# A two-layer attention and mixture-of-experts kernel: transposes in place of identity products, one-hot products on VectorE, expert numbers found earlier, loads of t ahead of a branch, more filler matmuls

## The chip, the core and the metric

The kernel runs on one core of one Trainium2 chip. The metric is the device time of one execution in microseconds (us); the time given is the median of several executions. A profile of one execution is read beside it. The engines are called as the profile calls them: PE is TensorE's matmul, PEld its weight load, DVE is VectorE, ACT is ScalarE, POOL is GpSimd, SP is SyncE, which here issues most DMAs.

## The reference

The input x is one image of 256 channels and 48 by 48 pixels, so 2304 tokens of 256 channels, all in float32. The reference computes:

```python
# layer 0: group norm, then softmax attention over tokens x heads (9216 rows of 64)
xt = gn(x).transpose(0, 2, 3, 1)
q, k, v = xt @ Wq.T + bq, xt @ Wk.T + bk, xt @ Wv.T + bv      # each as [9216, 64]
O = softmax(q @ k.T / 8, axis=1) @ v
x = x + (O.reshape(B, H, W, 256) @ Wo.T + bo)
# layer 1, attention through 64 slices
t = tokens(x); h = ln(t) @ W0 + b0
sw = softmax(h @ Ws + bs)                                      # [tokens, 64]
# q, k, v of h averaged over tokens with weights sw, attention among the 64 slices (8 heads of 32),
# result spread back to the tokens with sw, then @ Wout + bout
t = t + that
# layer 1, mixture of experts
xf = ln(t); top 2 of 8 experts by xf @ Wg, softmax over the two
for e in range(8): out += w_dense[:, e:e+1] * (gelu(xf @ W1[e] + b1[e]) @ W2[e] + b2[e])
t = t + out
```

The result is t as an image again, 256 by 48 by 48.

## The kernel before

The function `layers` computes everything and leaves t, one row a token, in a DRAM tensor `t_d`. The entry function calls it once, reads a flag `bad`, calls it again (with row maxima in the softmax) only if the flag is set, and then turns t into the image. Tile inserts the waits; operations issued through the small wrapper `InOrder` (`pe`, `dve`, `act`, `pool`; all of these show as L57) keep the order in which they are written on their engine, and those issued as `nc.tensor...` or `nc.vector...` may be moved by the scheduler.

**Projections.** x is loaded as [128, 2, 2304] (`x_sb`, channels on partitions). `transposed` turns a 256 by 256 weight with four PE transposes and copies the result with ACT. `Wq` and `Wk` are turned first; then DVE takes the statistics of x, PE sums them over groups with two small matmuls (`pg`, `pg2`) with DVE and POOL work between, one transpose `pb` turns the biases, and the normalized x (`xn`, which lies in the memory of `t_sb`) feeds the matmuls for q and k (L287, L291) in five blocks of tokens. The scheduler placed the transposes of `Wv` between `pb` and the first q matmul and those of `Wo` after the first block. The v matmuls (L316) follow.

**Attention.** 18 blocks of 512 rows of q run over 36 pairs of key tiles: `scores` (L57, `s<-q,kk`), an exponential on ACT, row sums on DVE, and `times_values` (`av<-p,v_sb`). `follow` puts the later steps of a finished token tile between two blocks: `out_proj` computes, in the PSUM tile `pa`, the output projection of the tile and adds x by multiplying `x_sb` with an identity; `turn`, `slices` and `gather` follow one block later each. The last two tiles are done after the loop, in tiles named `pm`. `busy(n, bank)` issues n matmuls [128x128] by [128x256] whose result nobody reads.

**Slices.** A chain of small matmuls and DVE/ACT steps between 64 slices ends in `tw`; two `busy(1, spin)` stand in it. Then each token tile gets its share added (`py`), with statistics, logits of the experts and the normalized t written to DRAM (`tn_d`).

**Routing.** DVE picks two experts for each token, counts them and gives each (token, expert) pair a slot in one of 43 tiles of 128 rows (`NSL`); each tile has one expert. The table from slot to token comes from one-hot products. For every column k of 36, `in_tile` (DVE, L57, 18 columns at a time) marks the tile, `what` (POOL, 9 columns at a time, 774 values) is `in_tile` times token and weight, `in_row` (DVE, 9 columns, 1152 values, printed as `t_sb<-row,back` since it lies in that memory) marks the row; PE adds up the products in `pwide` (`pw<-what,t_sb`). After that DVE counts, for each tile, how many experts end before it (`past`, `ex`), writes `expert_i` and `used_i` (integers), and turns the table into `slot_t` and `slot_w`.

**Experts.** For each tile s, POOL gathers its 128 rows of `tn_d` (`rows`, L1060, `xs`), SP loads the expert's W1 (`load_w1`, L1070, 1 MB, two buffers), PE turns xs (`turn`), `first` makes 1024 hidden values with ACT's gelu, `second` the output, and POOL adds it into `t_d` with an indirect DMA (L1120). 36 tiles are always run; the other seven stand in nested branches on `used_i`. In the profiled execution 39 ran. `expert_of` reads `expert_i` into a register.

**End.** All engines read `bad` and branch. The branch not taken has a short path on each engine that waits for the engine's and its DMA queues' counts and then raises them to what the skipped part would have left. Then SP loads t in five blocks of up to 512 tokens (`tt<-t_d`), PE turns them (L1209), DVE and ACT copy (`ob`), SP stores. The pool `fin` has five buffers of `tt` and five of `ob`.

Of the kernel before, what the change touches and what calls it, by code (L numbers as in the profile page):

```python
# [9 lines left out]
FP = mybir.dt.float32  # L10
# [5 lines left out]
P = 128  # L16
C = 256
# [26 lines left out]
def bc(ap, shape):  # L44

    return ap.unsqueeze(2).to_broadcast(shape)
# [16 lines left out]
def layers(  # L63
# [168 lines left out]
    with proj, tc.tile_pool(name="ps_pj", bufs=5, space=PSUM) as ps_pj, tc.tile_pool(  # L232
        name="ps_w", bufs=2, space=PSUM
    ) as ps_w:
        def transposed(dst, raw):
            pw = ps_w.tile([P, 2, C], FP, name="pw", tag="pw")
            for ci in range(2):
                for co in range(2):
                    nc.tensor.transpose(
                        pw[:, ci, co * P : (co + 1) * P], raw[:, co, ci * P : (ci + 1) * P], ident  # L240
                    )
            nc.scalar.copy(dst, pw)
            return dst

        WqT = transposed(pj.tile([P, 2, C], FP, name="WqT"), raws["Wq"])
        WkT = transposed(pj.tile([P, 2, C], FP, name="WkT"), raws["Wk"])

# [8 lines left out]
        nc.tensor.matmul(pg[:, 0:2], gm, mv[:, :, 0], start=True, stop=True)  # L256
# [7 lines left out]
        nc.tensor.matmul(pg2[:, 0:2], gm, dm, start=True, stop=True)  # L264
# [4 lines left out]
        nc.tensor.transpose(pb[:, 0:76], brow, ident[0:76, 0:76])  # L269
        nc.vector.tensor_copy(bcol, pb[:, 0:76])  # L270
        bq8 = pj.tile([P, 2], FP, name="bq8")
# [108 lines left out]
    def out_proj(i, ps):  # L380

        tok = slice(i * P, (i + 1) * P)
        g, u = divmod(i, TG // P)
        for c in range(2):
            pe.matmul(
                ps[:, 0:C], OT[:, g % 2, c, u * P : (u + 1) * P], WoT[:, c, :],
                start=(c == 0), stop=False,
            )
        for c in range(2):
            pe.matmul(  # L390
                ps[:, c * P : (c + 1) * P], x_sb[:, c, tok], ident, start=False, stop=(c == 1)
            )

        def add():
            dve.tensor_tensor(t_sb[:, i, 0:C], ps[:, 0:C], bo_bc, ALU.add)

        def spread():
            s6 = small.tile([P, 6], FP, name="s6", tag="s6")
            dve.bn_stats(s6, t_sb[:, i, 0:C])
            dve.bn_aggr(stats[:, i, :], s6)  # L400
            ve = small.tile([P, 1], FP, name="ve", tag="ve")
            dve.tensor_scalar(ve, stats[:, i, 1:2], 1e-5, None, ALU.add)
            pool.tensor_tensor(rstd_t[:, i : i + 1], ve, mhalf[:, 0:1], ALU.pow)
            return ve

        def norm():
            dve.tensor_scalar(
                tn[:, i % 6, :], t_sb[:, i, 0:C], stats[:, i, 0:1], rstd_t[:, i : i + 1],
                ALU.subtract, ALU.mult,
            )  # L410

        return [(2, add), (3, spread), (7, norm)]
# [69 lines left out]
    def attention():  # L482


        with tc.tile_pool(name="pexp", bufs=5) as pexp, tc.tile_pool(
            name="att", bufs=2
# [231 lines left out]
    with tc.tile_pool(name="sa", bufs=1) as sa:  # L718
        tw = sa.tile([P, C + E], FP, name="tw")
        with sums_done, tc.tile_pool(name="ps_b", bufs=3, space=PSUM) as ps_b, tc.tile_pool(  # L720
# [81 lines left out]
            for v in range(2):  # L802
                pa = ps_b.tile([S, 2, P], FP, name="pa", tag="mm")
                for u in range(2):
                    pe.transpose(pa[:, u, :], a[:, v, u, :], ident)
                if v == 0:
                    dve.tensor_copy(aT[:, v], pa)
                else:
                    act.copy(aT[:, v], pa)
            dve.tensor_reduce(am, a, AX.X, ALU.add)  # L810
            dve.reciprocal(am, am)
            pk = ps_b.tile([P, 4, D1], FP, name="pk", tag="mm")
            for v in range(2):
                for u in range(2):
                    for w in range(2):
# [4 lines left out]
                        )  # L820
            tok_sb = sa.tile([P, 4, D1], FP, name="tok_sb")
# [34 lines left out]
        with tc.tile_pool(name="ps_y0", bufs=7, space=PSUM) as ps_y0, tc.tile_pool(  # L856
            name="norm", bufs=2
# [40 lines left out]
    with gating, tc.tile_pool(name="onehot", bufs=1) as oh, tc.tile_pool(  # L898
# [100 lines left out]

        for k in range(0, K, G):  # L1000
# [3 lines left out]
            pool.tensor_tensor(  # L1004
# [6 lines left out]
            )  # L1011
        for j in range(K):
# [7 lines left out]

        past = gp.tile([P, NSL, E], FP, name="past")
        dve.tensor_tensor(
            past, bc(steps[:, 0:NSL], [P, NSL, E]), ends.unsqueeze(1).to_broadcast([P, NSL, E]), ALU.is_ge
        )
        ex = gp.tile([P, NSL], FP, name="ex")
        dve.tensor_reduce(ex, past, AX.X, ALU.add)
        dve.tensor_scalar(expert_i, ex[0:1, :], float(E - 1), None, ALU.min)
        dve.tensor_scalar(used_i, ends[0:1, E - 1 : E], float(NSL), None, ALU.min)
# [147 lines left out]
def kernel(ctx: ExitStack, tc: tile.TileContext, *args):  # L1176
    nc = tc.nc
    out_v = args[-1][0].rearrange("(c p) h w -> p c (h w)", p=P)
    both = ctx.enter_context(tc.tile_pool(name="both", bufs=1))
    bad = both.tile([1, 1], mybir.dt.int32, name="bad")  # L1180
    ident = both.tile([P, P], FP, name="ident")
# [3 lines left out]
    layers(tc, bad, ident, t_d, *args[:-1])  # L1185
    again = nc.values_load(
# [4 lines left out]


    sp = InOrder(tc, nc.sync)
    with tc.tile_pool(name="fin", bufs=len(TBLOCKS)) as fin, tc.tile_pool(
        name="ps_f", bufs=4, space=PSUM
    ) as ps_f:
        tts = []
        for t0, n in TBLOCKS:
            tt = fin.tile([P, 4, C], FP, name="tt", tag="tt")
            tts.append(tt)  # L1200
            sp.dma_start(
                out=tt[:, 0 : n // P, :], in_=t_d[t0 : t0 + n, :].rearrange("(i p) c -> p i c", p=P)
            )
# [48 lines left out]
```

## Time and profile before

| | us |
|---|---|
| median of 3 executions | 1629.55 |
| lowest, highest | 1628.57, 1630.72 |
| profiled execution | 1630.58 |
| its span, first to last instruction | 1628.8 |

| engine | busy us | share of the span |
|---|---|---|
| PE | 1573.0 | 97% |
| DVE | 1047.5 | 64% |
| ACT | 810.4 | 50% |
| POOL | 149.7 | 9% |

Approximate stages in the profiled execution: projections until 66 us, attention until 1243, slices until 1282, routing until 1317, experts until 1605, end until 1628.8. Busy time counts an instruction from start to end; PE's instructions overlap, so the spacing of starts tells the cost better than the duration. PEclk (and "granted clock") is the share of full TensorE clock that the chip granted. An arrow in a line names what ended the idle time before it.

### The profile page before, as it was taken

How to read it: one execution, taken by the hardware profiler on the slowest of the kernel's cores; microseconds unless marked ns; L12 is line 12 of the kernel's file. 1: busy time of each engine (PE TensorE's matmuls, PEld its weight loads, DVE VectorE, ACT ScalarE, POOL GpSimd, SP SyncE). 2: the span in 40 equal slices, each digit the busy share in tenths (PEclk: the TensorE clock that was granted, in tenths of full speed). 3: DMA queues.
4: the chain of work that ended last, by engine and by line, in shares of the span. 5: the costliest groups of instructions: out<-in, count | busy, mean ns of one | idle time of the engine just before them, and what ended most of it. 6: DMA issues, size and time to landing. Idle time of an engine off the chain costs nothing.

```text
span 1628.8 us, 31884 instructions
## 1 busy us (share of the span) xinstructions
PE 1573.0 (97%) x13244; PEld 792.2 (49%) x13244; DVE 1047.5 (64%) x1364; ACT 810.4 (50%) x1100; POOL 149.7 (9%) x129
## 2 busy tenths in 40 slices
PE   7999999999999999999999999999999689999995
PEld 3633343333333333333333333333345479999994
DVE  6577778777787887877878878778786721111111
ACT  2355565555555655655556556555553322333321
POOL 0000000000000000000000000000000253333321
PEclk9999999999999999999999999999999799999998
DMA  4000000000000000000000000000003656666655
GB/s 136 1 1 1 1 1 1 1 1 1 1 1 1 2 1 2 1 1 2 1 1 1 1 1 1 1 1 1 1 2 117 232 180 190 173 183 188 172 161 174
DMA packets 39877, 79.26 MB, mean 49 GB/s; under 512 B 3581, under 2 KB 26186, under 8 KB 39594
## 3 DMA queue, kind: packets, MB, share of 16 engines
q1 hardware_dynamic: 32042, 66.35, 12.1%
q0 software_dynamic: 7680, 10.75, 3.7%
q8 instruction: 108, 1.77, 0.4%
q14 instruction: 47, 0.39, 0.1%
HBM read 64.64 MB, written 12.45 MB: 47 GB/s over the span
## 4 chain that ended last, share of the span: by engine, by line
PE 92%; DVE 3%; DMA 2%; issue 1%; POOL 1%; ACT 0%; SPq 0%; ACTq 0%; POOLq 0%; DVEq 0%
PE s L57 34%; PE av L57 34%; PE ph L57 8%; PE py L57 8%; PE pa L57 2%; DMA t_d<-y,slot_t 2%; PE pb L57 1%; PE pp L287 1%; PE pp L316 1%; PE pp L291 1%; PE pt L57 1%; POOL what L57 0%; DVE s L57 0%; DMA Wq_raw<-in_L_conv_Wq_dram 0%; ACT p L57 0%
## 5 line engine op out<-in xcount | busy, mean ns | idle before, releaser
L57 DVE TENSOR_TENSOR acc<-acc,p 128x1024 f32<-128x1024 f32 x612 | 748.0, 1222 | 256.4 <-ACT p L57 248.3
L57 ACT ACTIVATE p<-s 128x1024 f32<-128x1024 f32 x648 | 662.9, 1023 | 493.3 <-PE s L57 483.2
L57 PE MATMUL av<-p,v_sb 64*64 64x512 f32 x5184 | 675.8, 590 | 1.4 <-ACT p L57 0.7
L57 PE MATMUL s<-q,kk 64*64 64x512 f32 x5184 | 674.9, 589 | 0.0
L57 PEld LDWEIGHTS s<-q,kk 64*64 64x64 f32 x5184 | 201.9, 133 | 351.3 <-issue 181.0
L57 PEld LDWEIGHTS av<-p,v_sb 64*64 64x64 f32 x5184 | 195.8, 131 | 358.1 <-ACT p L57 202.5
L57 ACT ACTIVATE hid<-ph,bcol 128x128 f32<-128x128 f32 x312 | 89.2, 368 | 220.0 <-PE ph L57 209.7
L57 PEld LDWEIGHTS ph<-xT,w 128*128 128x128 f32 x1248 | 147.7, 195 | 2.8 <-DVE xT L57 0.9
L57 PE MATMUL ph<-xT,w 128*128 128x128 f32 x1248 | 148.1, 278 | 0.5 <-DVE xT L57 0.5
L57 PE MATMUL py<-w_sb,hid 128*128 x624 | 147.1, 379 | 0.0
L57 POOL TENSOR_TENSOR rstd_t<-ve,mhalf 128x1 f32<-128x1 f32 (+1 forms) x21 | 27.6, 1312 | 1241.9 <-DVE ve L57 1241.9
L57 DVE COPY xT<-pt 128x256 f32<-128x256 f32 x40 | 17.0, 425 | 175.9 <-PE pt L57 168.6
L57 PEld LDWEIGHTS py<-w_sb,hid 128*128 128x128 f32 x624 | 112.8, 190 | 12.2
L1120 POOL DMA_INDIRECT t_d<-y,slot_t x39 | 61.7, 1583 | 98.7 <-DVE y L57 88.3
L57 DVE TENSOR_TENSOR y<-py,b_bc 128x256 f32<-128x256 f32 x39 | 16.6, 425 | 68.6 <-PE py L57 68.6
L1060 POOL DMA_INDIRECT xs<-tn_d,slot_t x36 | 38.3, 1064 | 91.5 <-PE pt L57 83.5
L57 DVE RECIPROCAL rinv<-pb 128x256 f32<-128x256 f32 x18 | 31.5, 1751 | 0.0
L57 DVE TENSOR_TENSOR acc<-p 128x1024 f32<-128x1024 f32 x18 | 22.1, 1225 | 8.4 <-ACT p L57 8.4
L304 DVE TENSOR_SCALAR q<-pp,bcol 64x512 f32<-64x512 f32 (+1 forms) x30 | 20.8, 694 | 8.6 <-PE pp L287 8.3
L57 DVE TENSOR_REDUCE up<-av 128x512 f32<-128x1024 f32 x18 | 21.9, 1217 | 0.0
L287 PE MATMUL pp<-t_sb,WqT 128*128 128x512 f32 (+1 forms) x40 | 19.0, 600 | 0.3 <-DVE t_sb L278 0.3
L1209 PE MATMUL pt<-ident,tt 128*128 128x128 f32 x36 | 5.8, 340 | 12.8 <-DMA tt<-t_d 12.8
(258 smaller groups left out, 616.6 us busy)
## 6 DMA issues: line engine op xcount, KB each, us to landing
w<-in_L_ffn_W_dram SPq DMA_DIRECT2D x40, 1024.0 KB
w_sb<-in_L_ffn_W_dram SPq DMA_DIRECT2D x8, 1024.0 KB
x_sb<-in_x_dram SPq DMA_DIRECT2D x4, 576.0 KB
t_d<-t_sb SPq DMA_DIRECT2D x3, 768.0 KB
tn_d<-tn SPq DMA_DIRECT2D x3, 768.0 KB
tt<-t_d SPq DMA_DIRECT2D x4, 512.0 KB
out_dram<-ob SPq DMA_DIRECT2D x4, 512.0 KB
b_bc<-in_L_ffn_b_dram SPq DMA_DIRECT2D x1, 1024.0 KB
```

The costliest lines, as they stand in the source:

```text
L57: return self.tc.keep_in_program_order(getattr(self.engine, name)(*args, **kwargs))
L287: nc.tensor.matmul(pq[:, 0:tn], WqT[:, c, cols], xn[:, c, toks], start=(c == 0), stop=(c == 1))
L291: nc.tensor.matmul(pk[:, 0:tn], WkT[:, c, cols], xn[:, c, toks], start=(c == 0), stop=(c == 1))
L304: nc.vector.tensor_scalar(dst, pq[rows, 0:tn], bcol[rows, B_Q + m : B_Q + m + 1], 0.125, ALU.add, ALU.mult,)
L316: nc.tensor.matmul(pv[:, 0:C], xn[:, c, i * P : (i + 1) * P], WvT[:, c, :], start=(c == 0), stop=(c == 1),)
L1060: nc.gpsimd.indirect_dma_start(out=xs, out_offset=None, in_=tn_d[:, :], in_offset=bass.IndirectOffsetOnAxis(ap=slot_t[:, s : s + 1], axis= ...
L1120: nc.gpsimd.indirect_dma_start(out=t_d[:, :], out_offset=bass.IndirectOffsetOnAxis(ap=slot_t[:, s : s + 1], axis=0), in_=y, in_offset=None ...
L1209: nc.tensor.transpose(pt[:, k * P : (k + 1) * P], tt[:, k, c * P : (c + 1) * P], ident)
```

## The change

- `transposed` and the small matmuls of the projections go through `pe`, so PE runs them in the written order: the transposes of Wv and Wo both stand after the first block. `busy_first` adds one filler matmul after `pg` and two after `pb`, into a PSUM bank of its own.
- `out_proj` turns x with two PE transposes that open the accumulation, and the projection is added after.
- Two more `busy(1, spin)` in the slices' chain: after the transposes of `a`, and after `pk`.
- `what` is computed on DVE. The experts' numbers are found inside that loop, on one partition: one DVE compare after the first nine columns, then three adds and two copies on POOL.
- The loads of t are issued before `bad` is read, and again inside the branch. `ob` has three buffers.
- Pools are smaller in the second call of `layers`, which isn't run with these inputs.

```diff
@@ projections
-                    nc.tensor.transpose(
+                    pe.transpose(
                         pw[:, ci, co * P : (co + 1) * P], raw[:, co, ci * P : (ci + 1) * P], ident
...
+        spun = ps_spun.tile([P, 256], FP, name="spun")
+        def busy_first(n):
+            for _ in range(n):
+                pe.matmul(spun, ident, raws["Wq"][:, 0, :], start=True, stop=True)
...
-        nc.tensor.matmul(pg[:, 0:2], gm, mv[:, :, 0], start=True, stop=True)
+        pe.matmul(pg[:, 0:2], gm, mv[:, :, 0], start=True, stop=True)
+        busy_first(1)
...
-        nc.tensor.transpose(pb[:, 0:76], brow, ident[0:76, 0:76])
+        pe.transpose(pb[:, 0:76], brow, ident[0:76, 0:76])
         nc.vector.tensor_copy(bcol, pb[:, 0:76])
+        busy_first(2)
@@ out_proj
+        for c in range(2):
+            pe.matmul(
+                ps[:, c * P : (c + 1) * P], x_sb[:, c, tok], ident, start=(c == 0), stop=False,
+                is_transpose=True,
+            )
         for c in range(2):
             pe.matmul(
                 ps[:, 0:C], OT[:, g % 2, c, u * P : (u + 1) * P], WoT[:, c, :],
-                start=(c == 0), stop=False,
-            )
-        for c in range(2):
-            pe.matmul(
-                ps[:, c * P : (c + 1) * P], x_sb[:, c, tok], ident, start=False, stop=(c == 1)
+                start=False, stop=(c == 1),
             )
@@ slices
+            busy(1, spin)
             dve.tensor_reduce(am, a, AX.X, ALU.add)
...
+            busy(1, spin)
             tok_sb = sa.tile([P, 4, D1], FP, name="tok_sb")
@@ routing
+        past = gp.tile([1, NSL, E], FP, name="past")
+        pool.memset(past, 0.0)
+        def find_experts():
+            dve.tensor_tensor(
+                past[:, :, 0 : E - 1], bc(steps[0:1, 0:NSL], [1, NSL, E - 1]),
+                ends[0:1, 0 : E - 1].unsqueeze(1).to_broadcast([1, NSL, E - 1]), ALU.is_ge,
+            )
+            for n in (4, 2, 1):
+                pool.tensor_tensor(past[:, :, 0:n], past[:, :, 0:n], past[:, :, n : 2 * n], ALU.add)
+            pool.tensor_copy(expert_i, past[:, :, 0])
+            pool.tensor_copy(used_i, ends[0:1, E - 1 : E])
         for k in range(0, K, G):
...
-            pool.tensor_tensor(
+            dve.tensor_tensor(
                 what[:, ks], in_tile[:, ks, :].unsqueeze(2).to_broadcast([P, G, 2, NSL]),
...
+            if k == 0:
+                find_experts()
...
-        past = gp.tile([P, NSL, E], FP, name="past")
-        dve.tensor_tensor(
-            past, bc(steps[:, 0:NSL], [P, NSL, E]), ends.unsqueeze(1).to_broadcast([P, NSL, E]), ALU.is_ge
-        )
-        ex = gp.tile([P, NSL], FP, name="ex")
-        dve.tensor_reduce(ex, past, AX.X, ALU.add)
-        dve.tensor_scalar(expert_i, ex[0:1, :], float(E - 1), None, ALU.min)
-        dve.tensor_scalar(used_i, ends[0:1, E - 1 : E], float(NSL), None, ALU.min)
@@ end
+    tts = [both.tile([P, n // P, C], FP, name=f"t{t0}") for t0, n in TBLOCKS]
+    def load_t():
+        for (t0, n), tt in zip(TBLOCKS, tts):
+            sp.dma_start(out=tt, in_=t_d[t0 : t0 + n, :].rearrange("(i p) c -> p i c", p=P))
+    load_t()
     again = nc.values_load(
         bad, min_val=0, max_val=1, skip_runtime_bounds_check_because="it is the result of a comparison"
     )
     with tc.If(again > 0):
         layers(tc, None, ident, t_d, *args[:-1])
-    with tc.tile_pool(name="fin", bufs=len(TBLOCKS)) as fin, tc.tile_pool(
+        load_t()
+    with tc.tile_pool(name="fin", bufs=3) as fin, tc.tile_pool(
         name="ps_f", bufs=4, space=PSUM
     ) as ps_f:
-        tts = []
-        for t0, n in TBLOCKS:
-            tt = fin.tile([P, 4, C], FP, name="tt", tag="tt")
-            tts.append(tt)
-            sp.dma_start(
-                out=tt[:, 0 : n // P, :], in_=t_d[t0 : t0 + n, :].rearrange("(i p) c -> p i c", p=P)
-            )
```

## The prediction, on record before the changed kernel ran

> **What bounds the kernel now.** I read the page's chain first, then the timeline of the stages that the change touches, then their granted clock, then the end. By engine the chain is:
>
> ```profile
> PE 92%; DVE 3%; DMA 2%; issue 1%; POOL 1%; ACT 0%; SPq 0%; ACTq 0%; POOLq 0%; DVEq 0%
> ```
>
> PE carries the time. Over 66 to 1236 us the waits of PE add up to 1.1 us, so a PE instruction taken out of attention is its spacing saved. Outside attention other things end last. PE between two blocks:
>
> ```profile
> 713.09 0.61 PE L57 MATMUL pa<-ident,x_sb 128*128 128x128 f32 x4
> 713.53 0.38 PE L57 MATMUL pa<-ident,tn 128*128 128x128 f32 x2
> 713.75 0.61 PE L57 MATMUL pb<-Wl,tnT 128*128 128x128 f32 x4
> ```
>
> Two products with an identity are four records, started over 0.44 us; two transposes are two records, over 0.22 us. The clock, in windows of 3.41 us set on the edges at which it changed (columns: window; PE, PEld, DVE, ACT, POOL busy; granted clock; DMA share; GB/s):
>
> ```profile
> 12.35:15.77 3.42, 2.33 (x8) 1.72 (x9) 2.02 (x10) 0.73 (x2) 0.73 (x1) 1.00 0.55 135
> 15.77:19.18 3.41, 3.41 (x5) 1.34 (x5) 1.90 (x5) 0.00 (x0) 0.00 (x0) 1.00 0.75 234
> 1261.63:1265.04 3.41, 2.56 (x26) 1.42 (x26) 1.64 (x5) 1.15 (x3) 0.00 (x0) 1.00 1.09 348
> 1265.04:1268.45 3.41, 3.41 (x8) 2.35 (x10) 0.43 (x1) 0.00 (x0) 0.00 (x0) 0.50 1.09 350
> 1312.83:1316.24 3.41, 0.00 (x0) 0.00 (x0) 0.00 (x0) 0.00 (x0) 2.50 (x4) 1.00 1.02 413
> 1316.24:1319.66 3.42, 2.37 (x10) 1.97 (x11) 0.42 (x1) 0.00 (x0) 2.74 (x3) 0.50 0.57 183
> ```
>
> After a window with gaps the next is granted half the clock (1265, 1316). The 1.00 before 19.18 only means that no record stands there: the q matmuls start 0.853 us apart until 18.95 and 0.43 after. Routing and the first expert tile (SPq w: loads of W1):
>
> ```profile
> 1294.85 0.96 DVE L57 TENSOR_TENSOR in_tile<-first_slot,at_big 128x774 f32<-128x774 f32 x1
> 1295.73 3.91 DVE L57 TENSOR_TENSOR t_sb<-row,back 128x1152 f32<-128x1152 f32 x2
> 1296.04 4.95 POOL L57 TENSOR_TENSOR what<-in_tile,wk 128x774 f32<-128x774 f32 x2 [9.77 <-DVE in_tile L57]
> 1299.57 2.25 DVE L57 TENSOR_TENSOR in_tile<-first_slot,at_big 128x774 f32<-128x774 f32 x1
> 1308.97 15.91 SPq L1070 DMA_DIRECT2D w<-in_L_ffn_W_dram  x3
> 1310.35 1.34 POOL L1060 DMA_INDIRECT xs<-tn_d,slot_t  x1 [3.37 <-DVE slot_w L57]
> 1317.98 6.25 PE L57 MATMUL ph<-xT,w 128*128 128x128 f32 x32 [0.52 <-DVE xT L57]
> ```
>
> DVE and POOL exclude each other: the first in_row runs 1.35, the second 2.64, ending 1.21 after POOL's first what (1298.43); in_tile takes 0.96 alone and 2.25 behind POOL. So the loop is serial: 12.1 us from 1294.85 to 1306.98, of which 1.34 for each what. And the first gather, issued at 1310.35, lands at 1316.7, when two loads of W1 issued since 1308.97 have drained (1316.5). PE stands idle 4.0 us, goes to half clock, and the first tile takes 6.25 where later ones take 3.73. The end:
>
> ```profile
> 1612.16 2.78 SPq L57 DMA_DIRECT2D tt<-t_d  x5
> 1616.54 5.82 PE L1209 MATMUL pt<-ident,tt 128*128 128x128 f32 x36 [12.81 <-DMA tt<-t_d]
> 1619.24 4.76 SPq L57 DMA_DIRECT2D out_dram<-ob  x5
> ```
>
> By the semaphore records the last scatter lands at 1608.52, but SP is let go only at 1611.53: POOL's branch at 1606.96 is followed by its next instruction at 1609.94, and it raises the scatters' counts until 1611.57. The loads land at 1616.13, 1617.57, 1619.22, 1620.72, 1621.40; PE starts with the first. The stores land from 1622.70 to 1627.16.
>
> **The change, part by part**, against the profiled execution's own 1630.58 us (span 1628.8); that execution lies 1.0 above the median, inside the spread of the runs.
>
> *Projections, -1.0.* The fillers close PE's gaps 12.30-13.14 and 13.96-15.37 (the second held Wv's transposes). Then 12.35-15.77 is full, and full clock should come about one window earlier. The four records from 15.37 to 18.95 at 0.853 instead of 0.43 are 1.8 too long. Against that: Wv's four transposes move to busy time, 4 x 0.109 = 0.4, and two fillers (four cold records of 256 columns, 0.43 each) run until about 15.55, 0.2 past 15.37. Left: -1.1; bounds -1.8 and +0.6 (no gain in clock).
>
> *x by transposes, -4.0.* (0.446 - 0.223) x 18 tiles; 16 lie in full PE time, the last two on the chain to t_sb. Bounds -4.2, -3.6. [...]
>
> *Fillers in the slices, -0.7.* They fill 0.4 us each before pk and before tok_sb's transpose, both within waits for DVE and ACT (aT at 1263.16, tok_sb at 1264.13), and end with these. If 1265.04-1268.45 then keeps full clock, pw's four records start 0.22 apart instead of 0.44: 0.9 saved, and DVE waits for tw. I take three quarters. Bounds -1.2, +0.3.
>
> *Routing and first tile, -5.7.* DVE alone now has 2 in_tile x 0.88, 4 what x 0.88, 4 in_row x 1.27, one compare 0.4: 10.8 us. POOL's five small steps are bounded by its 128x6 product, 0.20, and by a what, 1.34 for 774 values; at 172, 86, 43, 43 and 1 values I take 1.6 in all, and as POOL excludes DVE, they add: the loop ends at 1307.2, as before (1305.7 if they cost DVE nothing). So moving what gains nothing by itself. But expert_i is there at about 1303.8 instead of 1308.1: POOL's steps alternate with DVE's. SP's loads move from 1308.97 to 1304.7 and have drained (7.5 us, as now) at 1312.3. The gather is issued at 1310.6 and, free of them, lands 1.34 + 1.9 later (gathers after the drain land 1.5 to 1.9 after their issue ends): 1313.8 instead of 1316.7, -2.9. The fillers (busy(8)) end 5.6 after the loop, 1312.8, so PE idles 1 us instead of 4.0 and keeps its clock, as it did with 52% busy at 1295.77-1299.18: 6.25 becomes 3.6 and the turn 0.3 less, -3.0, of which I count 2.8. Bounds: -9 (POOL free) and -1.5 (still cold, gather still queued).
>
> *Loads ahead of the verdict, +2.0.* SP needs only the scatters: the loads start at about 1608.8, 3.3 earlier. But in the built program SP's not-taken path raises the DMA counts queue by queue, waiting for each of the five loads first, and PE's first transpose waits for a count raised after the fifth. The last load lands at 1608.8 + 9.2 = 1618.0; PE starts at about 1618.5 instead of 1616.54, cold. First store 2.7 later, 1621.2; landings 3.3 after that and then 4.5 for the other four as now: 1629.0; the fourth ob waits for the first store, about 0.3 more. 1629.2 against 1627.16. The branch itself (3.0 to 4.7 us on the engines) is hidden by the loads; uncovered it costs up to 3 more. Bounds -3.3 (PE starts with the first load) and +4.
>
> Sum: -1.0 - 4.0 - 0.7 - 5.7 + 2.0 = -9.4, so 1621.2 for an execution like the profiled one, 1620.2 from the median. I say 1620.5.
>
> **The rivals.**
> *The first tile stays cold or the gather stays queued* (for it: a window 75% busy, at 1261.63, did lose the clock): that part gives -1.8, the sum 1624.5.
> *The early loads pay in full*, if PE isn't held to the fifth load: -3.3 for +2.0, 1615.2. Against: the waits in the program.
> *Only the transposes work*: -4.0, the clock in projections and slices unmoved (+0.6), the tile -1.8, the end +4: about 1629, within 0.2% (3.3 us, about what a measurement of this kernel can tell from no change).
> *Slower: POOL's steps.* They stand between DVE's, and each blocks it. If each costs as much as a what as seen on POOL's line, 2.5 us, five are 12.5, the loop ends at 1318 and the gather lands at 1324.7, 8 later than now: -1.0 - 4.0 - 0.7 + 8 + 2.0 = +4.3, 1634. It decides from 1.7 us each. For it: no one-partition step of POOL on the profile, and 1.33 for its power at 128x6. Against: 0.20 to 0.30 for product and scaling at 128x6.
>
> **How the numbers follow.** Forecast 0.62, cold or queued 0.16, loads in full 0.10, only transposes 0.06, POOL slower 0.06. The range takes the forecast's bounds and the two nearest rivals, 1615.0 to 1626.0. Faster: the first three, 0.88; same: 0.07 with the edge of the second; slower 0.05. [...]
>
> **What would show it.** In the profile after: x's transposes two records within 0.23; q matmuls 0.43 apart from about 15.8; pw under 1.3 us; what at 0.9 to 1.0 on DVE, W1's loads issued before the loop ends; PE idle before the first xs about 1 us and ph x32 at 3.7; the loads of t under 0.6 us after the scatter, PE's first transpose after the fifth. It is wrong if PE waits in attention, if POOL's steps exceed 1 us each, or if PE starts its last transposes with the first load.

## The result, and the profile after

The changed kernel took 1627.07 us in the median of four executions (1625.11 to 1628.46), the kernel before, on the same chip, 1630.13. The ratio is 0.9982, with a 95% interval of 0.9964 to 0.9999. So it is some 3 us faster, not 9.4; the time lies above the range that was given.

The profiled execution took 1625.11 (span 1623.3) and is the fastest of the four. On its page the chain that ended last covers only the last microseconds (0% by every engine), so the stages are read one by one from the timeline. PE between two blocks of attention, first the line of the kernel before that stood ahead of x's products, then the changed kernel:

```profile
712.12 1.13 PE L57 MATMUL pa<-WoT,OT 128*128 128x256 f32 x4
```

```profile
708.75 0.44 PE L57 MATMUL pa<-ident,x_sb 128*128 128x128 f32 x2
709.03 1.03 PE L57 MATMUL pa<-WoT,OT 128*128 128x256 f32 x4
709.89 0.38 PE L57 MATMUL pa<-ident,tn 128*128 128x128 f32 x2
```

From the first start of this group to the first `pa<-ident,tn` it was 1.41 us (712.12 to 713.53) and is 1.14: 0.27 less, a little more than the 0.223 of the forecast. A record is the entry of one instruction in the profile. The first record after attention is followed later than the same record elsewhere: the large product by 0.10 (0.32 instead of 0.22), the small transpose by 0.06 (0.17 instead of 0.11).

From one change of the granted clock to the next this trace has 1262.93 (from 13.43 on), 10.24, 20.48, 6.83, 283.31, 17.07 and 6.83 us, each a whole number of windows of 3.413. The clock in such windows, set on the edges at which it changed in this execution (columns as before: window; PE, PEld, DVE, ACT, POOL busy; granted clock; DMA share; GB/s):

```profile
13.43:16.84 3.41, 2.83 (x12) 1.66 (x12) 2.48 (x8) 0.00 (x0) 0.73 (x1) 1.00 0.60 98
1259.29:1262.70 3.41, 3.31 (x20) 2.32 (x19) 1.47 (x4) 0.00 (x0) 0.00 (x0) 1.00 1.09 348
1303.66:1307.08 3.42, 0.72 (x4) 0.29 (x2) 0.00 (x0) 0.00 (x0) 2.51 (x4) 1.00 0.66 247
1307.08:1310.49 3.41, 2.71 (x11) 2.31 (x12) 0.42 (x1) 0.00 (x0) 2.80 (x3) 0.50 0.39 114
```

In the slices full clock now holds (1.00, where it was 0.50): the window of 1259.29 lies where the one of 1265.04 lay before, 26.9 us after the pause ahead of the last two tiles. Before the first expert tile PE is idle most of a window (busy 0.72 of 3.42 us, before 0.00 of 3.41), and the next window runs at half, as it did. Routing and the first tile:

```profile
1287.08 0.96 DVE L57 TENSOR_TENSOR in_tile<-first_slot,at_big 128x774 f32<-128x774 f32 x1
1290.76 5.69 POOL L57 TENSOR_TENSOR past<-past 1x172 f32<-1x172 f32 x3 [11.95 <-DVE past L57]
1296.51 0.86 POOL L57 CAST expert_i<-past 1x43 int32<-1x43 f32 x1
1297.34 1.30 POOL L57 CAST used_i<-ends 1x1 int32<-1x1 f32 x1
1298.16 21.79 SPq L1091 DMA_DIRECT2D w<-in_L_ffn_W_dram  x4
1302.66 1.34 POOL L1081 DMA_INDIRECT xs<-tn_d,slot_t  x1 [4.02 <-issue]
1307.26 0.69 PE L57 MATMUL pt<-ident,xs 128*128 128x128 f32 x2 [2.88 <-DMA xs<-tn_d,slot_t]
1308.47 6.42 PE L57 MATMUL ph<-xT,w 128*128 128x128 f32 x32 [0.52 <-DVE xT L57]
```

The loads of W1 are issued 11.1 us after the first `in_tile` (14.1 before). The first gather is issued 15.58 after it, where it was 15.50: no earlier. Its rows come 20.2 after it (21.9 before), PE has waited 2.88, and `ph` takes 6.42 (6.25 before). The end, first the last scatter of the kernel before, then the changed kernel:

```profile
1604.86 1.56 POOL L1120 DMA_INDIRECT t_d<-y,slot_t  x1 [5.49 <-DVEq L1167]
```

```profile
1595.40 1.56 POOL L1141 DMA_INDIRECT t_d<-y,slot_t  x1 [5.49 <-DVEq L1188]
1600.91 3.51 SPq L57 DMA_DIRECT2D t<-t_d  x5
1611.57 5.43 PE L1232 MATMUL pt<-ident,t 128*128 128x128 f32 x36 [17.30 <-SPq L1221]
```

PE's first transpose of t waits for SP at the branch (L1221) and starts 16.2 us after the last scatter's issue, where it was 11.7 (1604.86 to 1616.54).

One table holds all profiles, each row one execution. The columns: until PE's pause of 0.3 us at about 133 us (projections and two blocks); from there to the pause of 0.9 ahead of the last two tiles (before `pb<-both,ones`); from there to the end of the slices; then from the first `in_tile` to the first rows at PE; from there to the first scatter's issue; to the last scatter's; to PE's first transpose of t; to the end. What lies between the slices and `in_tile` is taken as 14.8 in all of them.

| kernel | to 133 | attention | slices | to rows | to 1st scatter | experts | to t | to end | span |
|---|---|---|---|---|---|---|---|---|---|
| before | 133.2 | 1104.98 | 41.86 | 21.93 | 16.05 | 272.03 | 11.68 | 12.29 | 1628.8 |
| b_same | 134.2 | 1104.98 | 40.39 | 22.13 | 15.36 | 272.03 | 11.38 | 12.39 | 1627.7 |
| b_loads | 133.5 | 1104.99 | 40.39 | 22.02 | 15.44 | 272.03 | 15.08 | 12.24 | 1630.5 |
| b_turns | 132.2 | 1100.64 | 39.87 | 21.83 | 15.46 | 272.03 | 11.73 | 12.40 | 1621.0 |
| b_routing | 132.9 | 1104.98 | 41.73 | 19.60 | 17.28 | 271.92 | 11.33 | 12.55 | 1627.1 |
| b_fill | 132.8 | 1104.98 | 40.41 | 21.93 | 16.16 | 272.03 | 11.38 | 12.60 | 1627.1 |
| after | 131.8 | 1100.63 | 39.90 | 20.18 | 16.22 | 271.92 | 16.17 | 11.69 | 1623.3 |
| a_again | 133.8 | 1100.64 | 39.90 | 20.20 | 16.29 | 271.92 | 16.23 | 11.75 | 1625.5 |
| a_loads_behind | 133.9 | 1100.64 | 39.90 | 20.31 | 16.22 | 271.91 | 12.16 | 12.86 | 1622.7 |
| a_nobranch | 133.3 | 1100.63 | 39.91 | 20.34 | 17.98 | 272.93 | 8.10 | 12.77 | 1620.8 |
| g_one_ahead | 133.6 | 1100.64 | 39.91 | 20.19 | 19.70 | 271.92 | 10.00 | 16.15 | 1626.9 |
| a_fill14 | 133.1 | 1100.64 | 39.91 | 20.28 | 15.29 | 271.92 | 15.67 | 12.23 | 1623.8 |
| c_steps_dve | 133.1 | 1100.64 | 39.91 | 19.47 | 19.29 | 271.92 | 11.73 | 12.06 | 1622.9 |
| f_late_fill14 | 133.7 | 1100.64 | 39.92 | 20.27 | 13.39 | 275.82 | 11.71 | 12.29 | 1622.6 |
| f_all2 | 133.6 | 1100.63 | 39.92 | 20.41 | 13.34 | 274.12 | 11.73 | 12.51 | 1621.1 |
| f_all | 133.4 | 1100.63 | 39.92 | 20.41 | 13.34 | 274.15 | 12.48 | 12.16 | 1621.3 |
| h_pool | 133.1 | 1100.64 | 39.92 | 20.19 | 13.39 | 271.92 | 11.72 | 12.59 | 1618.3 |
| h_best | 133.5 | 1100.65 | 39.92 | 19.50 | 13.39 | 271.92 | 11.69 | 12.26 | 1617.7 |

Attention repeats within 0.02 us as long as its code is the same, and so do the experts, but for `a_nobranch`, which takes 1.0 more there with the same code. So what is worth a part of these two can be read from its column to a tenth, where the whole time scatters by 2 or 3. The columns around the first tile scatter more.

### The profile page after: what moved, and what is told of

Read it like the earlier page. It is cut to its first block, busy times and chain, and to the rows that moved or that the text cites. A ratio compares the mean times of both kernels' runs of the same rounds, so it can differ in the third digit from the quotient of the medians.

```text
span 1623.3 us, 31835 instructions
## 1 busy us (share of the span) xinstructions
PE 1565.4 (96%) x13218; PEld 785.3 (48%) x13218; DVE 1045.4 (64%) x1365; ACT 810.4 (50%) x1100; POOL 147.7 (9%) x131
## 5 line engine op out<-in xcount | busy, mean ns | idle before, releaser
L57 PEld LDWEIGHTS py<-w_sb,hid 128*128 128x128 f32 x624 | 112.7, 190 | 12.2
L1081 POOL DMA_INDIRECT xs<-tn_d,slot_t x36 | 38.3, 1065 | 90.4 <-PE pt L57 82.1
L1232 PE MATMUL pt<-ident,t 128*128 128x128 f32 x36 | 5.4, 325 | 17.3 <-SPq L1221 17.3
L57 DVE TENSOR_REDUCE up<-av 128x512 f32<-128x1024 f32 x18 | 21.9, 1216 | 0.0
L297 PE MATMUL pp<-t_sb,WqT 128*128 128x512 f32 (+1 forms) x40 | 17.2, 552 | 0.6 <-DVE t_sb L288 0.6
```

The lines of the kernel that those rows point to most:

```text
L57: return self.tc.keep_in_program_order(getattr(self.engine, name)(*args, **kwargs))
L297: nc.tensor.matmul(pq[:, 0:tn], WqT[:, c, cols], xn[:, c, toks], start=(c == 0), stop=(c == 1))
L1081: nc.gpsimd.indirect_dma_start(out=xs, out_offset=None, in_=tn_d[:, :], in_offset=bass.IndirectOffsetOnAxis(ap=slot_t[:, s : s + 1], axis= ...
L1232: nc.tensor.transpose(pt[:, k * P : (k + 1) * P], tt[:, k, c * P : (c + 1) * P], ident)
```

## The experiments

The theory after the first profile of the changed kernel: the transposes pay in full; routing gives 1.6 of 5.7; and the loads in front cost 4. The rival: the late start of t was an accident of one execution. All times below are medians; the time of the kernel before, taken beside each group, follows in brackets.

**The end.** The changed kernel once more, unchanged:

> The changed kernel unchanged, once more, timed in more rounds and profiled a second time. Theory (the loads of t cost their time in every execution): 1627 us, 3 under the kernel before; in the profile the first transpose of t starts about 16 us after the issue of the last scatter (before 11.7), since SP's way past the branch lies behind its five loads; everything up to that scatter is about 9.5 earlier than before. Rival (the late scatter and the slow branch were an accident of the one profiled execution): the first transpose starts 13.6 us after the issue, as the prediction had it, and the time in more rounds is about 2 lower, 1625.

1626.48 (1629.64), ratio 0.9982 (0.9973 to 0.9991), and PE's first transpose again 16.2 after the last scatter's issue. No accident. But that scatter is issued 7.3 earlier than in the kernel before, not 9.5: the other 2.1 came from the early clock of the first profile, in the projections (131.8 against 133.8), and that was luck. Next, the end of the kernel before put back:

```diff
-    load_t()
     again = nc.values_load(bad, ...)
     with tc.If(again > 0):
         layers(tc, None, ident, t_d, *args[:-1])
-        load_t()
-    with tc.tile_pool(name="fin", bufs=3) as fin, ...
+    with tc.tile_pool(name="fin", bufs=len(TBLOCKS)) as fin, ...
+        for t0, n in TBLOCKS:
+            tt = fin.tile([P, 4, C], FP, name="tt", tag="tt")
+            sp.dma_start(out=tt[:, 0 : n // P, :], in_=t_d[t0 : t0 + n, :].rearrange(...))
```

> The changed kernel with the end of the kernel before: the loads of t behind the branch, five buffers of ob. Theory: the loads in front cost 4 us, so 4 less than the changed kernel, about 1623, 7 under the kernel before; the first transpose 11.7 us after the last scatter's issue. Rival 1 (the prediction's price of +2): 1625. Rival 2 (the end is no loss on average, and the gain went elsewhere): 1627, as the changed kernel.

1621.96 (1629.64), ratio 0.9953 (0.9939 to 0.9967). That is 4.5 under the changed kernel: near the theory's 4, not the prediction's 2. The other way round, the kernel before with that part alone (the smaller pools of the second pass come with it):

```diff
+    load_t()
     again = nc.values_load(bad, ...)
     with tc.If(again > 0):
         layers(tc, None, ident, t_d, *args[:-1])
+        load_t()
```

> The kernel before with the loads of t in front of the branch, nothing else (with the smaller pools of the second pass that this needs). Theory: the first transpose of t 16 us after the last scatter's issue instead of 11.7, the end 4 later: +4, 1634. Rival 1 (the prediction): 13.6 and +2, 1632. Rival 2 (the cost came with the other parts): 0.

1633.2 (1629.97), ratio 1.0019 (1.0010 to 1.0028): 3.2 slower, between the theory's 4 and the prediction's 2, and alone it makes a slower kernel. The lines of its end:

```profile
1603.21 1.56 POOL L1120 DMA_INDIRECT t_d<-y,slot_t  x1 [5.49 <-DVEq L1167]
1607.39 3.12 SPq L57 DMA_DIRECT2D t<-t_d  x5
1618.29 7.00 PE L1211 MATMUL pt<-ident,t 128*128 128x128 f32 x36 [16.21 <-SPq L1200]
```

The loads are issued 4.2 us after the scatter instead of 7.3, but PE starts 15.1 after it. By the semaphore records the fifth load lands 14.85 after it, 0.23 ahead of PE: PE waits for the fifth load, as the program says. What the loads gain in their start they partly lose on the way: from the first issue to the last landing 10.0 to 11.1 us in the four profiles with five loads in front of a branch, 9.1 to 9.9 with the loads behind it.

How much of it is the branch? Two kernels ask that: one leaves the branch and the second pass out of the program, the other puts one load in front and four behind.

```diff
 # a_nobranch
-    again = nc.values_load(bad, ...)
-    with tc.If(again > 0):
-        layers(tc, None, ident, t_d, *args[:-1])
-        load_t()
 # g_one_ahead
-    load_t()
+    load_t(0, 1)
...
-        load_t()
+        load_t(0, 1)
+    load_t(1, 5)
```

> The changed kernel with the verdict's branch and the second pass behind it left out; the loads of t stay as they are. Theory (SP's way past the branch, with the code fetched among the loads' transfers and a wait for each load's count, holds PE's first transpose): PE starts with the first load, about 9 us after the last scatter's issue instead of 16, the end is some 6 us earlier, 1620.5. Rival (the loads themselves are the slow part): PE starts 13 after the issue or later, and the time is within 3 of the changed kernel.

1621.79 (1630.19), ratio 0.9944 (0.9931 to 0.9958). PE starts 8.1 after the last scatter's issue, with the first load: from that scatter to the end it is 7.1 shorter than in `a_again`. In the medians the changed kernel is 3.2 under the kernel before and this one 8.4, so 5.2 of the 7.1 arrive; the profile lost 1.7 in the first tile and 1.0 in the experts, which this edit doesn't explain. With no branch behind them the same five loads take 9.8 from the first issue to the last landing: a sign, from one profile, that the branch is what lengthens them.

> The changed kernel with one of the five loads of t in front of the branch and four behind it. Theory 1 (the code behind the branch is fetched through the same DMA engines and waits behind the loads' packets): with 0.5 MB in front instead of 2.4 SP's branch takes 4.8 us as in the kernel before, instead of 6.1 to 7.1, and PE's first transpose starts 10.3 after the last scatter's issue. Theory 2 (the branch takes 6 to 7 us in this place whatever is being moved): 12.3. By both the four loads behind it land later than in the kernel before, so the end is no better than with all five behind: 1622 to 1624.

1627.82 (1629.55), ratio 0.9988 (0.9979 to 0.9997).

```profile
1610.71 1.94 PE L1233 MATMUL pt<-ident,t 128*128 128x128 f32 x8 [11.13 <-SPq L1221]
```

PE starts 10.0 after the scatter, as theory 1 had it. The time misses both theories' 1622 to 1624: the end takes 16.2 from PE's start, 1.7 less in all than in the changed kernel, and the first tile lost 3.4 in the profile. SP's way past the branch, from its compare to its next instruction, took 4.3 to 4.75 us in the kernels with the loads behind, where it lies 10.5 us ahead of the last scatter and costs nothing; 5.9, 6.1, 7.0 and 7.1 with five loads in front of it; 4.2 with one. In the changed kernel's trace the next block of code is moved at 1609.16 (8 KB in an instruction queue), 4.3 us after SP's compare, while the loads' packets are under way. So the branch took 5.9 to 7.1 us behind 2.4 MB of loads and 4.2 to 4.75 elsewhere. That this block of code waits behind the loads' packets was not shown by itself. Either way its end and the fifth landing fall within 0.2 us of each other in three of the four profiles (1.2 apart in `b_loads`), so neither alone is the whole cost.

**The transposes**, alone on the kernel before (the diff of `out_proj` as in the change):

> The kernel before with x turned by transposes, nothing else. Theory: two records of 0.11 us for four in each of 18 tiles, -4.0 us against the kernel before. [...] Rival 2 (the saving falls into waits for ACT's exponentials between two blocks): -1 or less.

1624.37 (1629.64), ratio 0.9968 (0.9956 to 0.9980): -5.3, faster than the whole change, and rival 2 is out. In the table attention is 4.34 shorter (16 tiles at 0.27) and the slices 0.5 (two tiles), 4.9 together.

**The fillers** of projections and slices, alone on the kernel before, and the kernel before profiled again:

> The kernel before with the fillers alone: PE's written order and three fillers in the projections, two in the slices. Theory (the clock's windows fall anywhere; the profiled execution of the kernel before had a lapse at 1265 that another one without these fillers did not have): projections unchanged within 1 us, slices 39.9 us from pm's gap to their end, as they are without a lapse, so 0 to -1 in the median. Rival (the prediction): -1.0 in the projections and -0.7 in the slices, -1.7.

> The kernel before, profiled a second time. Theory (the lapse of the clock at 1265 is an accident of the window's position): slices 40.4 or 41.9 us from pm's gap to their end, projections until 69.2 to 70.2, as in the kernels with these parts unchanged. Rival (it belongs to the kernel): 41.9 again.

`b_fill` 1629.68 (1630.19), ratio 0.9996 (0.9987 to 1.0005); `b_same` is one execution, 1629.44. The column to 133 us averages 133.2 over the five kernels without the fillers (132.2 to 134.2) and 133.3 over the thirteen with them (131.8 to 133.9): nothing gained. The reason is not that the fillers left gaps. `a_again` is the same program as the changed kernel, and in it they close the window that the prediction wanted closed:

```profile
12.25:15.66 3.41, 3.41 (x12) 2.54 (x11) 1.49 (x7) 0.59 (x1) 0.73 (x1) 1.00 0.55 180
15.66:19.07 3.41, 3.41 (x6) 1.52 (x5) 2.45 (x7) 0.00 (x0) 0.00 (x0) 1.00 1.01 341
```

PE is busy for all 3.41 us, and the window after it still runs at half clock: its q products start 0.85 apart until 18.54 and 0.43 apart from 19.24 (the 1.00 means again that no record of the clock stands there before 19.07). Nine of the thirteen profiles with the fillers have such a full window ahead of one at half clock. In `after` the window 10.01:13.43, with nearly the same instructions and PE busy 3.39, was followed by full clock, from 13.43 on. What decides is not shown. On average full clock begins at 17.2 with the fillers and at 19.2 without, and attention's first `s<-q,kk` starts 0.4 earlier (67.8 against 68.3). That is lost again: six of the thirteen have a window at half clock that begins between 67.2 and 68.5, none of the five has one, and it costs 1.05 (66.03 instead of 64.97 from that `s<-q,kk` to the pause at 133). Ahead of it, too, PE was busy without a gap: 3.41 us of 64.66:68.07 in `h_best`, most of it small products of weights.

The slices lose 1.4 us in two of the five kernels without fillers (41.9 and 41.7 against 40.4, or 39.9 where x is turned) and in none of the thirteen with them. By chance alone two such lapses would both fall on these five in 10 of 153 cases. So these two fillers most likely do what they are for, and it is worth 0.6 on average; the median of `b_fill` can't tell that from nothing.

**Routing**, alone on the kernel before (the diff of routing as in the change):

> The kernel before with the changed routing alone: one-hot values on DVE, the experts' numbers found inside the loop. Theory (two profiles of the changed kernel): slot_w 0.6 us earlier and the first rows of xs at PE 1.65 earlier, counted from the first in_tile; the gather itself is issued no earlier, since POOL now waits for DVE one instruction sooner; so -1.6 us against the kernel before. Rival 1 (the prediction): -2.9 for the gather, and -5.7 if PE keeps its clock. Rival 2 (the earlier loads of W1 only stand in the way of the gather): 0 or slower.

1629.55 (1630.19), ratio 1.0002 (0.9993 to 1.0011): nothing that can be measured. Its profile has the rows at PE 2.3 earlier, and then:

```profile
1320.53 1.03 PE L57 MATMUL py<-w_sb,hid 128*128 x4
1323.55 2.72 PE L57 MATMUL ph<-xT,w 128*128 128x128 f32 x22 [1.99 <-issue]
```

2.0 us of PE idle between the first two tiles, put down to nothing that the profile shows. The next kernel takes away the idle time ahead of the first tile, with six more fillers in the changed kernel:

```diff
-        busy(8, spin)
+        busy(14, spin)
```

> The changed kernel with 14 instead of 8 fillers behind the routing's products, so that PE works until the first rows of xs land. Theory (PE's 2.9 us of idle time inside one clock window cost the next window its full clock): PE idle under 1.5 us before the first transpose of xs, ph x32 3.7 us instead of 6.4, the time 2.7 less than the changed kernel, 1624.4. Rival 1 (half clock comes from something else, or the fillers hold xT up): ph x32 stays over 6 us, the time 1627 or more. Rival 2 (it depends on where the window's edge falls): the profile shows the one or the other, and the median lies between, at 1625 to 1626.

1626.13 (1629.64), ratio 0.9979 (0.9969 to 0.9988): 0.35 under the changed kernel, where 2.7 were expected.

```profile
1309.67 3.84 PE L57 MATMUL ph<-xT,w 128*128 128x128 f32 x32 [0.52 <-DVE xT L57]
1313.56 1.01 POOL L1081 DMA_INDIRECT late_xs<-tn_d,slot_t  x1 [0.30 <-issue]
1316.19 1.01 POOL L1081 DMA_INDIRECT xs<-tn_d,slot_t  x1 [0.31 <-issue]
1320.28 0.44 PE L57 MATMUL pt<-ident,xs 128*128 128x128 f32 x2 [1.68 <-DMA xs<-tn_d,slot_t]
```

The clock is kept and `ph` takes 3.84, just as the prediction wanted. But PE then waits 1.68 for the third tile's rows: their gather is the tenth in POOL's queue, behind seven `late_xs` for tiles that run 250 us later, and each takes POOL 1.3 us. It also comes behind the third load of W1 (issued at 1313.54): the gathers issued after that land 4.0 to 6.0 us after their issue, those just before in 2.8. In the changed kernel it is the eighth and ahead of that load, and the first tile takes longer at half clock; whether that order would have been late at full clock is not shown.

The small steps on DVE (from here on with the loads of t behind the branch):

```diff
-                pool.tensor_tensor(past[:, :, 0:n], past[:, :, 0:n], past[:, :, n : 2 * n], ALU.add)
-            pool.tensor_copy(expert_i, past[:, :, 0])
-            pool.tensor_copy(used_i, ends[0:1, E - 1 : E])
+                dve.tensor_tensor(past[:, :, 0:n], past[:, :, 0:n], past[:, :, n : 2 * n], ALU.add)
+            dve.tensor_copy(expert_i, past[:, :, 0])
+            dve.tensor_copy(used_i, ends[0:1, E - 1 : E])
```

> The changed kernel with the loads of t behind the branch, and with the five small steps of the experts' numbers on DVE instead of POOL. Theory (what POOL's 7.9 us for five steps hold up is the loads of W1, which then stand before the gather in the DMA queues): the five steps take under 1 us on DVE, the first load of W1 is issued 5.5 us after the first in_tile instead of 11.1 and has drained before the gather is issued; xs is at PE 18.3 after in_tile instead of 20.2; 1.9 less than the same kernel with the steps on POOL, 1620. Rival 1 (the gather is slow by itself): no change, 1622. Rival 2 (five steps more on DVE lengthen the loop): +0.5.

1622.12 (1630.19), ratio 0.9949 (0.9936 to 0.9963); with the steps on POOL it was 0.9953. No gain that the medians show.

```profile
1292.09 0.86 DVE L57 TENSOR_TENSOR past<-past 1x172 f32<-1x172 f32 x3
1294.02 21.96 SPq L1091 DMA_DIRECT2D w<-in_L_ffn_W_dram  x3
1304.71 1.33 POOL L1081 DMA_INDIRECT xs<-tn_d,slot_t  x1 [24.52 <-DVE slot_w L57]
1307.92 0.44 PE L57 MATMUL pt<-ident,xs 128*128 128x128 f32 x2 [1.49 <-DMA xs<-tn_d,slot_t]
```

The three adds take 0.86 on DVE and 5.69 on POOL. W1's loads start 5.6 after `in_tile`, have drained before the gather, and the rows are at PE 3.2 after the gather's issue instead of 4.6. The first half of the theory holds, but for 0.8 us in the table instead of 1.9: the five steps now lengthen DVE's loop (12.2 for 11.5), and the gather is issued 0.7 later after `in_tile`, as rival 2 had it (+0.5). A stall of 4.0 between the first two tiles of this execution, like the one above, hides the rest in the profile.

Then the late gathers are held back: their slot numbers are copied to tiles of their own, all at the ninth tile (`f_`), or one in every second tile from the seventh on (`h_`). `f_all2` and `h_best` have the steps on DVE as well, and `f_all` a third buffer of W1 too; `h_best` has 11 fillers, the others 14.

```diff
 # h_pool
+        slot_late = [fp.tile([P, 1], mybir.dt.int32, name=f"slot_late{j}") for j in range(NSL - SURE)]
...
+            slots = slot_t[:, s : s + 1] if s < SURE else slot_late[s - SURE]
-                in_offset=bass.IndirectOffsetOnAxis(ap=slot_t[:, s : s + 1], axis=0),
+                in_offset=bass.IndirectOffsetOnAxis(ap=slots, axis=0),
...
+            if s >= 6 and s % 2 == 0 and (s - 6) // 2 < NSL - SURE:
+                j = (s - 6) // 2
+                dve.tensor_copy(slot_late[j], slot_t[:, SURE + j : SURE + j + 1])
```

> The changed kernel with the loads of t behind the branch, 14 instead of 8 fillers, and the rows of the seven tiles behind the sure 36 gathered later (their slot numbers are copied at the ninth tile), so that the third tile's rows are the third gather of POOL's queue and not the tenth. Theory (with the clock kept, the 1.7 us that PE then waited were for the third tile's rows, queued behind seven gathers of 1.3 us each): no gap of PE over 0.6 us behind the first rows, from PE's first rows to the first scatter 13.3 us instead of 16.2 (15.3 with the fillers alone), so 3 less than with the loads behind the branch alone: 1619. Rival 1 (W1's third load is what is late): the gap stays at 1.7, 1621. Rival 2 (the wait was an accident of one execution): the gap is gone, but 1621 as the median hardly moves.

> As the kernel with 14 fillers and late gathers, with the five small steps on DVE besides. Theory: the first rows reach PE 19.5 us after the first in_tile instead of 20.3, as the steps on DVE showed, and nothing behind them is late: 0.8 less, 1618. Rival 1 (the 4.0 us that PE lost in the first tile with the steps on DVE come with them): the gap is there again, 1621. Rival 2 (the gather's own time bounds): same, 1619.

> As the one with steps on DVE, 14 fillers and late gathers, with a third buffer of W1 and its load issued in front. Theory (W1 isn't late once the gathers are): no change, 1618, or some tenths more if the third load is still under way when the first gather is issued. Rival (the third load of W1 is late by up to 1.7 us): 1616.5.

1622.64, 1621.8 and 1622.22 (1629.55), ratios 0.9957 (0.9944 to 0.9971), 0.9950 (0.9937 to 0.9964) and 0.9950 (0.9936 to 0.9963). From the rows to the first scatter it is 13.3 to 13.4, as the theory said, 2.9 less than in the changed kernel. All the same the three miss their theories' times by some 4. The experts after the first scatter take 274 to 276 instead of 272, and the loss stands where the seven gathers now run in a row, from 1375 on: PE idles 1.9 to 2.0 at 1387, and in `f_late_fill14` a window at half clock follows at 1389. PE waits there for DVE's copy `xT`, which comes 4.0 to 4.1 after the transposes that it copies, where 0.42 is usual. The rows of that tile had been gathered 14 us before, so it is not they that are late; by which way the gathers hold this up is not shown. 14 fillers end after the rows have landed once the steps are on DVE (20.4 to the rows, not 19.5), and a third buffer of W1 changes nothing. Spread out:

> The changed kernel with the loads of t behind the branch, 14 fillers, and the seven late gathers spread, one in every second tile from the seventh on. Theory (the third tile's rows in POOL's queue were what took the kept clock's gain away, and seven late gathers in a row cost PE 2 us at 1387): 13.4 us from PE's first rows to the first scatter, 272 from there to the last scatter as in the changed kernel, so 3 less than with the loads behind the branch alone: 1619. Rival (a gather more per tile is too much for POOL): 274 or more, 1621.

> The same with the five small steps on DVE and 11 fillers, so that the fillers end when the rows land. Theory: the first rows reach PE 19.4 us after the first in_tile, 13.4 to the first scatter, 272 to the last, 24 to the end; 1618, 1 less than with the steps on POOL. Rival (the stall of 2 to 4 us in the first tile that one kernel with the steps on DVE showed belongs to them): 1620 or more.

1619.98 and 1619.37 (1629.97), ratios 0.9939 (0.9925 to 0.9952) and 0.9930 (0.9916 to 0.9943). The experts are back at 271.92. `h_best`:

```profile
1308.39 0.44 PE L57 MATMUL pt<-ident,xs 128*128 128x128 f32 x2 [0.23 <-DMA xs<-tn_d,slot_t]
1309.10 1.01 POOL L1084 DMA_INDIRECT xs<-tn_d,slot_t  x1 [1.31 <-PE pt L57]
1309.34 3.84 PE L57 MATMUL ph<-xT,w 128*128 128x128 f32 x32 [0.52 <-DVE xT L57]
1318.11 0.38 PE L57 MATMUL pt<-ident,xs 128*128 128x128 f32 x2
```

The third tile's rows are gathered as soon as the first's are turned, and PE waits for nothing. At 10.6 under the kernel before it is the fastest of all. From `in_tile` to the first scatter it takes 32.9, 4.8 less than the 37.7 of the old routing on average: what the prediction expected of routing (-5.7) is nearly there once the steps, the fillers and the order of the gathers are all changed.

## Why the prediction was wrong

The sum was -9.4, the time moved by -3.1. By its own terms:

- **Projections, forecast -1.0: 0.** The step that failed is "Then 12.35-15.77 is full, and full clock should come about one window earlier". The window became full, as `a_again` shows, and the next one still ran at half. There the fillers, at half clock themselves, also hold the first q product until 15.98 (15.37 before). Full clock came 2 us earlier on average, not 3.4, and the window at half clock at 67 to 72 took the gain back. That it began at 13.4 in `after` was luck, the earliest of the thirteen profiles; in `a_again` it began at 19.1, in the five without the fillers at 17.3 to 20.7. The bound of +0.6 stood for no gain in clock; the forecast still counted the gain. The first edges of `after` and `a_again`, 13.43 and 19.07 us from the first instruction of the same program, lie 5.64 apart, not a whole number of windows of 3.41: in these two executions the windows lay differently against the program.
- **x by transposes, forecast -4.0: -4.9** in the columns, -5.3 in the median. Right in its mechanism; 0.27 a tile and not 0.223, since a small record right after attention loses 0.06 and a large one 0.10.
- **Fillers in slices, forecast -0.7: -0.6** on average. Right, as far as two lapses in 18 profiles can tell.
- **Routing and first tile, forecast -5.7: -1.2** (36.4 to 36.5 from `in_tile` to the first scatter in the three profiles without the stall, 37.3 to 38.1 in the five with the old routing). Where the stall strikes, the same routing takes 36.9, 38.3 and 39.9 (`b_routing`, `a_nobranch`, `g_one_ahead`); over all six it gains 0.2, and the median of `b_routing` shows no gain at all. This is the largest error. The loop did gain, 11.5 us for 12.1, where none was expected. Three steps failed. POOL's five steps were taken at 1.6 and took 7.9 from the first's start to the last's end, so W1's loads came 11.1 after `in_tile` and not 9.9. The gather was issued 4.1 after the loop's end, not 3.4: the trace has POOL waiting for DVE at an instruction ahead of the gather. So the gather found W1's loads still under way, where the prediction had it free of them: its rows were at PE 4.6 after its issue, not 3.2, and PE idled 2.9 instead of 1. So the clock was lost, as the first rival said. And behind that was a wait that no step of the prediction named: with the clock kept, the third tile's rows were late in `a_fill14`. The order of POOL's gathers was in the trace of before: the third tile's rows were the eighth, behind five `late_xs`.
- **Loads ahead of the verdict, forecast +2.0: +4.0** in the columns (27.9 for 23.9), +4.5 and +3.2 by the two comparisons. The mechanism was right: PE waits for the fifth load, which `b_loads` shows, where the branch ends 1.2 before it. Mis-sized were the start of the loads, 4.1 to 5.5 after the scatter's issue instead of 3.9, and their passage, 10.0 to 11.1 instead of 9.2. The branch, taken at 3.0 to 4.7 and hidden, took 5.9 to 7.1 and ended with the fifth load in three of four profiles. The bound of +4 for this step held in the columns; the forecast was half of it.

Sum by the columns: 0 - 4.9 - 0.6 - 1.2 + 4.0 = -2.7, against -3.1 and -3.2 measured. With the 0.2 of all six profiles for routing it would be about -1.7, so the 1.2 fits better, but the sum doesn't prove it. The rival of a cold tile had the right mechanism and still used -1.8 and +2.0 for the two large parts, so its 1624.5 was 2.5 short. The slower rival (POOL's steps) was wrong as it was built: three adds take 1.9 each, above its threshold of 1.7, but DVE's steps beside them took at most 0.3 longer (one `what` 1.20 instead of 0.95), so they block little; they delay `expert_i`. That DVE and POOL exclude each other, as the prediction read from the large steps of the kernel before, does not hold for these small ones.

Open: the stall of 1.6 to 4.0 us of PE between the first two tiles in four of the profiles (`b_routing`, `c_steps_dve`, `a_nobranch`, `g_one_ahead`), whose cause is not shown. The profile names DVE's copy `xT` in three of them, and in all four that copy comes 2.3 to 5.2 after its transposes instead of 0.42, the same picture as at 1387 in the `f_` kernels. In both places a run of late gathers is under way or just over, and the two kernels that spread them show no stall; that is a hint and no proof. Open too: why a window with PE busy throughout did not bring or keep full clock; why the gather's issue follows `slot_w` later in the new loop; and why the loads of t take longer ahead of a branch.

## What to carry to other kernels

Before a removed wait is counted as a gain, look for the next arrival in the same queue: in `a_fill14` seven gathers that nobody needed yet stood ahead of one that was needed, and PE's wait of 1.68 us for it showed only when the clock was kept. A load moved ahead of a branch is only worth its lead if nothing behind the branch waits for all of its queue; otherwise the branch, hidden until then, joins the path: in `after` the loads started 5.5 us after the last scatter's issue instead of 7.3, and PE 16.2 after it instead of 11.7. A term that depends on where a clock window falls is worth its average over executions, not what one profile shows: full clock began at 13.4 us in `after` and at 19.1 in `a_again`, the same program. And that PE is busy through a window, by the profile's records, is not yet a reason to count on full clock in the next: in `a_again` it was busy 3.41 of 3.41 us, and the q products behind it started 0.85 apart until 18.54.

## What the runs showed that was not expected

- Small steps on one partition: three adds of 172, 86 and 43 values took 3.3, 0.9 and 1.3 us on POOL beside a busy DVE, 5.69 with the gaps (`after`); on DVE 0.86 together (`c_steps_dve`). A copy of a single value took 1.30 on POOL and 0.13 on DVE.
- The branch that is not taken, over the whole second pass, took SP 5.9 to 7.1 us behind 2.4 MB of loads and 4.2 to 4.75 elsewhere.
- A window in which PE was busy throughout was followed by one at half clock: 12.25:15.66 in `a_again`, 64.66:68.07 in `h_best`.
- The order of POOL's gathers differs between builds that differ in fillers alone: the third tile's rows were the eighth gather in one and the tenth in the other.
